# Group-norm statistics moved between slices, and the last image's loads regrouped, in a dilated attention and binary convolution kernel

## The chip, the cores and the metric

The kernel runs on one core of one Trainium2 chip. The metric is the device time of one execution in microseconds (us). A profiled execution has a span, from its first to its last instruction, and a time of its own that is a little longer. TensorE (PE in the profile) multiplies matrices, VectorE (DVE), ScalarE (ACT) and GpSimd (POOL) work elementwise, and SyncE (SP) issues most DMAs. PEld is TensorE's loading of weights.

## What is computed

Input and output are 16 images of 56 x 56 pixels with 384 channels in float32. Two layers follow each other, each with a group norm ahead of it and a residual around it:

```python
x = x + _L0_conv_ref(_gn(x), L0_conv_w_qkv, L0_conv_w_proj, L0_conv_b_proj)
x = x + _L1_conv_ref(_gn(x), L1_conv_w)
```

`_gn` takes mean and variance over all pixels of one image and the 12 channels of each of 32 groups. So no pixel of an image can be normalised before the whole image has been seen:

```python
g = v.reshape(B_, H_, W_, G, C_ // G)
m = jnp.mean(g, axis=(1, 2, 4), keepdims=True)
s = jnp.var(g, axis=(1, 2, 4), keepdims=True)
return ((g - m) / jnp.sqrt(s + eps)).reshape(v.shape)
```

Layer 0 projects to q, k and v (384 to 1152 channels), lets each pixel attend to 3 x 3 neighbours in 3 groups of 4 heads, with dilations 1, 2 and 3 in the groups, and projects back with a bias. Layer 1 is a depthwise 3 x 3 convolution whose weights are clipped and turned to their signs.

## The kernel before

The work is cut into 112 chunks of 8 image rows (448 pixels), 7 per image. Channels lie on the partitions, in three groups of 128. Each chunk passes three plans. `plan_a` loads the input, transposes it, takes its statistics and writes it channel by channel to the scratch tensor `xd`. `plan_b` is layer 0: it normalises, projects q, k and v, forms nine products t with the keys on VectorE (`score`, L516), sums them on TensorE, takes the softmax, spreads the weights with TensorE, multiplies with v on VectorE and adds on GpSimd (`weigh`, L586 and L594), projects, adds the residual, takes layer 1's statistics and stores to `x1d`. `plan_c` is layer 1: it loads `x1d`, normalises, convolves and transposes to the output.

The order is written out by hand. Each piece of work is entered with a slice and an order in it (`at`, L382), the pieces are emitted sorted by both (L836), and a chunk starts every 9 slices (`STEP`, L820). The orders are listed at L819; SOFTMAX, SCORE, CONVOLVE, WEIGH and QUERY stand ahead of STATISTICS, then come QKV, PROJECT, the transposes, NORM and LOADS. This is the order in which pieces are written; VectorE and GpSimd are seen to depart from it in the trace, where an instruction whose input comes late is passed by later ones. [...]

**Statistics.** `group_norm` (L295) returns six steps that lie in different slices: `channels` (VectorE combines the chunks' statistics, L305), `mean` (a matmul and a scaling, L311 and L314), `deviation` (matmuls, VectorE L323, GpSimd L324 and L325), `variance` (a matmul and three VectorE operations, L331 to L338), `invert` (thirteen small GpSimd operations that find the inverse square root, L345 to L349, and leave `pair`), and `spread_out` (matmuls `pp`, L354, bring mean and scale back to the channels; for layer 1 more matmuls `pz`, L367, bring them to the layout of the convolution; VectorE copies both to `mr`, L358, and `mrz`, L372). Only `channels` and `invert` have no matmul. For layer 1 the steps lie in slices 0, 1, 2, 4, 5 and 7 after slice 27 of the image's last chunk (L822, L649), for layer 0 at the same offsets from another start (L821, L443).

**Layer 1 in an image.** The first 256 channels are convolved on TensorE: z holds a set of 32 channels three times on 96 partitions, once for each of three image rows shifted (`load`, L669), there are 4 sets for each j of 2, ScalarE normalises z with `mrz` (L701), and twelve taps per j accumulate (`convolve`, L709). The last 128 channels, g, are multiplied by their taps on ScalarE (`taps_g`, L762) and added on GpSimd (L768), after ScalarE has normalised `xg` to `zg` with `mr` (L740). `turn` (L778) transposes to the output; ScalarE copies it to `osb`, and a DMA stores that.

**The last image.** It has no later image to share the engines with, so `plan_c` treats it apart (L675 to L680 and L790 to L804). z lies in halves of two sets, in tiles that layer 0 has no use for any more: `t` tiles for even chunks, three `w` tiles and one `xn` tile for odd ones. VectorE normalises the fourth set (L697) and does the taps of g alone (`taps_last`, L753). Loads of z are by image row and half, six for each j (L688). Loads of xg (L729), from a pool of two `xg` tiles, and of x1 (L707), from a pool of two `x1` tiles, are entered six slices ahead of the chunk; the loads of z follow five and four slices ahead. SP issues all of these in one queue. An xg or x1 tile is free again when the chunk two back has been transposed to the output.

## Time and profile before

The median of three runs is 5430.9 us (5424.45 to 5435.38).

| | us |
|---|---|
| Profiled execution, its own time | 5427.23 |
| its span | 5425.5 |
| mean granted TensorE clock | 0.976 |
| `invert`, GpSimd L345 / L346 / L347, mean of one (96 of each in all) | 0.195 / 0.211 / 0.188 |
| `channels`, VectorE L305, mean of one (96 in all) | 0.337 |
| L594, GpSimd add of w, mean of one | 3.05 |
| L768, GpSimd add of taps, mean of one | 3.05 |
| L586, VectorE product w, mean of one | 1.55 |
| z load for one image row (L688), issue to landing, median | 4.0 |
| z_last load (last image), issue to landing, median | 3.5 |
| x1 load (L707), issue to landing, median | 7.9 |

The profile's page gives the busy time of each engine, the span in 40 slices of 135.6 us, the DMA queues, the chain that ended last, and the costliest groups. Its busy time of TensorE includes matmuls that run slower because the granted clock is lower. A timeline lists instructions in order: start, duration, engine, line, operation, tiles, and in brackets how long the engine had been idle and what ended that. In a table of stretches each row has a stretch's bounds and length, the busy time of PE, PEld, DVE, ACT and POOL with their instructions, the granted clock, the busy share of the DMA engines and the GB/s they moved. A line of waits names who waited, for whom, and then the sum in us, how often, and the longest.

### The profile page before, as it was taken

Reading aid. Unit: us, or ns where it says so; the run is one execution under the profiler, and the core shown is the slowest. Engines: PE = TensorE matmul, PEld = TensorE weight load, DVE = VectorE, ACT = ScalarE, POOL = GpSimd, SP = SyncE. Lnnn points to the kernel's source line nnn. Section 1 sums busy time; section 2 is a strip of 40 time slices with the busy share of each in tenths; the row PEclk is TensorE's granted clock in tenths of the full one; section 3 lists DMA queues with packets and bytes.
Section 4 is the critical chain, followed back from the end, with each engine's and each line's share of the span. In section 5 each row is a group of like instructions: output and inputs, shape, how many; then the busy total and the mean of one; then the engine's idle time right before and its main releaser. Section 6 shows DMA issues by size and latency. Waiting matters only on the chain. (4 is left out here: it accounts for less than half of the span.)

```text
span 5425.5 us, 77496 instructions
## 1 busy us (share of the span) xinstructions
PE 5215.6 (96%) x27669; PEld 2430.9 (45%) x27669; DVE 4143.1 (76%) x4209; ACT 2400.9 (44%) x4189; POOL 4216.7 (78%) x3049
## 2 busy tenths in 40 slices
PE   8999999999999999999999999999999999999965
PEld 4444444444444444444444444444444444444422
DVE  4887777878777787778877777787778878777753
ACT  3224444444444444444444444444444444444433
POOL 2677888888787887888888888887888888888870
PEclk9999999999999999999999999999999999999976
DMA  5444555655556555555655555555555555545444
GB/s 167 126 119 124 160 158 152 164 153 161 154 158 162 164 156 161 159 158 152 163 153 160 155 160 161 162 156 161 159 158 153 164 152 160 155 134 134 128 120 129
DMA packets 811640, 825.75 MB, mean 152 GB/s; under 512 B 360307, under 2 KB 801014, under 8 KB 811254
## 3 DMA queue, kind: packets, MB, share of 16 engines
q1 hardware_dynamic: 803270, 808.79, 54.2%
q10 hardware_dynamic: 7984, 12.00, 0.7%
q8 instruction: 219, 3.59, 0.3%
q14 instruction: 167, 1.37, 0.1%
HBM read 466.41 MB, written 231.21 MB: 129 GB/s over the span
## 5 line engine op out<-in xcount | busy, mean ns | idle before, releaser
L594 POOL TENSOR_TENSOR w<-w 128x1344 f32<-128x1344 f32 x672 | 2049.9, 3050 | 461.3 <-DVE w L586 359.3
L586 DVE TENSOR_TENSOR w<-pb_a,v 128x1344 f32<-128x1344 f32 x1008 | 1560.3, 1548 | 246.4 <-PE pb_a L579 164.6
L516 DVE TENSOR_TENSOR t<-pq,k 128x1344 f32<-128x1344 f32 x1008 | 1535.1, 1550 | 247.0 <-PE pq L463 247.0
L463 PE MATMUL pkv<-xn,wqkvT 128*128 128x448 f32 x3924 | 1565.6, 548 | 0.0
L463 PEld LDWEIGHTS pkv<-xn,wqkvT 128*128 128x128 f32 x3924 | 717.8, 190 | 659.4 <-issue 631.1
L612 PE MATMUL po<-y,wprojT 128*128 128x448 f32 x2016 | 833.3, 550 | 19.6 <-POOL y L598 15.7
L768 POOL TENSOR_TENSOR m<-m 128x1344 f32<-128x1344 f32 x210 | 640.0, 3048 | 272.2 <-ACT m L762 272.2
L463 PE MATMUL pq<-xn,wqkvT 128*128 128x448 f32 x1962 | 826.7, 557 | 0.0
L701 ACT ACTIVATE z<-z,mrz 96x448 f32<-96x448 f32 x840 | 578.4, 751 | 435.8 <-DMA z<-x1d 407.2
L501 PE MATMUL ps<-t,sel 128*32 128x448 f32 x6048 | 678.3, 559 | 35.4 <-DVE t L516 34.8
L762 ACT ACTIVATE m<-zg,ktap 128x448 f32<-128x448 f32 x945 | 554.0, 658 | 285.0 <-POOL m L768 278.0
L612 PEld LDWEIGHTS po<-y,wprojT 128*128 128x128 f32 x2016 | 376.3, 191 | 373.8 <-issue 343.5
L715 PE MATMUL pc<-z,kdiag 96*32 96x440 f32 (+1 forms) x5040 | 528.9, 554 | 6.1 <-POOL z L703 4.4
L722 DVE TENSOR_TENSOR x<-pc,x 128x448 f32<-128x448 f32 x224 | 139.8, 624 | 461.4 <-PE pc L715 461.3
L463 PEld LDWEIGHTS pq<-xn,wqkvT 128*128 128x128 f32 x1962 | 345.4, 189 | 311.3 <-issue 311.3
L579 PE MATMUL pb_a<-aT,spread 24*128 24x448 bf16 x3024 | 369.3, 360 | 41.0 <-DVE w L586 35.7
L598 POOL TENSOR_TENSOR y<-y,w 128x448 f32<-128x448 f32 x336 | 381.4, 1135 | 22.6
L597 POOL TENSOR_TENSOR y<-w 128x448 f32<-128x448 f32 x336 | 381.9, 1137 | 14.7
L473 ACT COPY v<-pkv 128x448 f32<-128x448 f32 x336 | 178.6, 531 | 474.5 <-PE pkv L463 466.2
L615 DVE SCALAR_TENSOR_TENSOR xr<-po,bias,xr 128x448 f32<-128x448 f32 x336 | 227.7, 678 | 187.3 <-PE po L612 183.4
L473 ACT COPY k<-pkv 128x448 f32<-128x448 f32 x336 | 178.2, 530 | 371.0 <-PE pkv L463 371.0
L501 PEld LDWEIGHTS ps<-t,sel 128*32 128x32 f32 x6048 | 172.4, 111 | 378.9 <-issue 250.4
(128 smaller groups left out, 4406.2 us busy)
## 6 DMA issues: line engine op xcount, KB each, us to landing
z<-x1d SPq DMA_DIRECT2D x570, 224.0 KB, 4.0
xr<-xd SPq DMA_DIRECT2D x112, 672.0 KB, 4.3
x1d<-xr SPq DMA_DIRECT2D x112, 672.0 KB, 3.2
xn<-xd SPq DMA_DIRECT2D x109, 672.0 KB, 4.6
xin<-in_x_dram SPq DMA_DIRECT2D x108, 672.0 KB, 7.1
xd<-xa SPq DMA_DIRECT2D x315, 224.0 KB, 3.5
out_dram<-osb SPq DMA_DIRECT2D x420, 168.0 KB, 3.4
x<-x1d SPq DMA_DIRECT2D x112, 448.0 KB, 7.9
```

What stands on the lines that cost most here:

```text
L463: nc.tensor.matmul(dst[:, :PX], wqkvT[:, cc, o0 : o0 + P], had["xn"][:, cc, :], start=(cc == 0), stop=(cc == NG - 1))
L501: return nc.tensor.matmul(had["ps"][32 * j : 32 * j + 32, :PX], sel[:, s0 : s0 + 32], tk, start=(issued[j] == 1), stop=(issued[j] == len(r ...
L516: nc.vector.tensor_tensor(t.rearrange("p k (r w) -> p k r w", w=W), q3, k3, ALU.mult)
L586: nc.vector.tensor_tensor(w.rearrange("p k (r w) -> p k r w", w=W), pb[:, :, :PX].rearrange("p k (r w) -> p k r w", w=W), three(kv[1][g][m ...
L594: nc.gpsimd.tensor_tensor(w0, w0, w, ALU.add)
L597: nc.gpsimd.tensor_tensor(y, w0[:, 0], w0[:, 1], ALU.add)
L598: nc.gpsimd.tensor_tensor(y, y, w0[:, 2], ALU.add)
L612: nc.tensor.matmul(po[:, :PX], wprojT[:, g, j * P : (j + 1) * P], had[f"y{g}"], start=(g == 0), stop=(g == NG - 1))
L701: nc.scalar.activation(z, z, AF.Identity, bias=mrz[:, j, q, 0:1], scale=mrz[:, j, q, 1:2])
L715: return nc.tensor.matmul(pcr[q * HD : (q + 1) * HD, :, lo:hi], kdiag[:, kx, j * NQ + q, :], rows(set_of(j, q))[:, :, lo + kx - 1 : hi + k ...
L762: nc.scalar.activation(rows(t[:, kx]), zp[:, ky : ky + ROWS, kx : kx + W], AF.Copy, scale=ktap[:, o : o + 1])
L768: nc.gpsimd.tensor_tensor(had["m"], had["m"], t, ALU.add)
```

## The change

Four things are changed. The orders gain one: STATISTICS now stands ahead of CONVOLVE, and a new order SPREAD stands where it was. `channels` and `invert` get STATISTICS, the four steps with matmuls get SPREAD, for both layers. The last step for layer 1, `spread_out`, lies one slice sooner. In the last image the load of x1 is entered three slices later, xg lies in an `xn` tile (of which there are three), and the half of odd chunks that lay in an `xn` tile lies in the `xr` tile. And in the last image's chunks 1 to 5 z is loaded by sets: one DMA brings all three image rows of a set, so there are four DMAs for each j where there were six. Its first and last chunk are loaded as before.

```diff
@@ plan_a
             for k in range(6):
-                at(t0 + 5 + STAT0_SLICE[k], STATISTICS, lambda k=k: norm(k))
+                at(t0 + 5 + STAT0_SLICE[k], STAT_ORDER[k], lambda k=k: norm(k))
@@ plan_b
             for k in range(6):
-                at(t0 + 27 + STAT1_SLICE[k], STATISTICS, lambda k=k: norm(k))
+                at(t0 + 27 + STAT1_SLICE[k], STAT_ORDER[k], lambda k=k: norm(k))
@@ plan_c, load
                 for q0 in range(0, NQ, 2):
-                    pool, tag = (t_p, "t") if c % 2 == 0 else (w_p, "w") if (j, q0) != (1, 2) else (xn_p, "xn")
+                    pool, tag = (t_p, "t") if c % 2 == 0 else (w_p, "w") if (j, q0) != (1, 2) else (xr_p, "xr")
...
                 for z, q0, q1 in had[f"z{j}"]:
+                    if b == B - 1 and 0 < c < NCH - 1:
+                        continue
                     nc.sync.dma_start(
                         z[ky * HD : (ky + 1) * HD, :, lo:hi], by_set[:, q0:q1, n0 + lo : n0 + hi]
                     )
+            if b == B - 1 and 0 < c < NCH - 1:
+
+                for q in range(NQ):
+                    one = by_set[:, q, p0 - W : p0 - W + PX]
+                    three_rows = bass.AP(one.tensor, one.offset, [(W, 3), *one.ap])
+                    nc.sync.dma_start(set_of(j, q), three_rows)
@@ plan_c, load_g
-            had["xg"] = xg = xg_p.tile([P, ROWS + 2, W], F32, tag="xg", name="xg")
+            if b < B - 1:
+                had["xg"] = xg = xg_p.tile([P, ROWS + 2, W], F32, tag="xg", name="xg")
+            else:
+                xg = xn_p.tile([P, NG, PX], F32, tag="xn", name="xg_last").rearrange("p j n -> p (j n)")
+                had["xg"] = xg = rows(xg[:, : (ROWS + 2) * W])
@@ plan_c, last image
             at(t0 - 6, LOADS, load_g)
-            at(t0 - 6, LOADS, load_x)
+            at(t0 - 3, LOADS, load_x)
@@ orders
-    SOFTMAX, SCORE, CONVOLVE, WEIGH, QUERY, STATISTICS, QKV, PROJECT, STAGE_A, STAGE_C, NORM, LOADS = range(12)
+    SOFTMAX, SCORE, STATISTICS, CONVOLVE, WEIGH, QUERY, SPREAD, QKV, PROJECT, STAGE_A, STAGE_C, NORM, LOADS = range(13)
+
+    STAT_ORDER = (STATISTICS, SPREAD, SPREAD, SPREAD, STATISTICS, SPREAD)
     STEP = 9
     STAT0_SLICE = (0, 1, 2, 4, 5, 7)
-    STAT1_SLICE = (0, 1, 2, 4, 5, 7)
+    STAT1_SLICE = (0, 1, 2, 4, 5, 6)
```

## The prediction

> **What bounds the kernel now.** I read the page first (busy shares, 40 slices), then the stretches by engine, then TensorE's waits in the middle, then the timeline around one of them, and last the DMA queue's waits in the end.

> ```profile
> span 5425.5 us, 77496 instructions
> ...
> PE 5215.6 (96%) x27669; PEld 2430.9 (45%) x27669; DVE 4143.1 (76%) x4209; ACT 2400.9 (44%) x4189; POOL 4216.7 (78%) x3049
> ...
> PE   8999999999999999999999999999999999999965
> ...
> PEclk9999999999999999999999999999999999999976
> ...
> 2848.00:3179.00 331.00, 326.08 (x1754) 153.01 (x1753) 259.54 (x263) 153.96 (x270) 271.95 (x192) 0.99 0.57 157
> ...
> 5320.00:5340.00 20.00, 11.96 (x60) 5.98 (x60) 8.24 (x13) 6.88 (x12) 0.00 (x0) 0.58 0.49 141
> ```

> In the middle TensorE (the first engine column of a stretch) is busy 98.5%; there, only less TensorE idling or a better granted clock (third column from the end) is time. In the last two slices every engine idles and the clock is near half. So there are two purses: the idling once per image, and the end.

> ```profile
> PE ps L501 <- DVE t L516: 29.4, 22, 2.0
> PE pb_a L579 <- DVE w L586: 24.3, 14, 7.1
> PE pv L331 <- POOL dev L325: 10.9, 14, 0.9
> ```
> ```profile
> 1131.91 0.37 PE L579 MATMUL pb_a<-aT,spread 24*128 24x448 bf16 x3 [1.34 <-DVE w L586]
> ...
> 1134.84 3.21 PE L501 MATMUL ps<-t,sel 128*32 128x448 f32 x16 [2.02 <-DVE t L516]
> ```
> ```profile
> 1134.86:1138.27 3.41, 3.41 (x20) 0.97 (x24) 1.93 (x2) 2.19 (x4) 2.70 (x2) 0.50 0.98 285
> ```

> From 100 to 5000 us TensorE waits some 75 us, 54 of them in the first two lines, at one place per image. The pair of 1.34 and 2.02 us, 3.36 us in sum, comes once in each of 13 images (the first has one wait of 7.1 us), always followed by a stretch at half clock: 3.41 us in nine images, 6.83 in four. At half rate half of it is lost: (9 x 3.41 + 4 x 6.83) / 2 / 13 = 2.2 us. One such place costs 5.6 us, and 13 cost 73.

> Its cause lies 30 us before. The timeline has ScalarE idle 4.50 us at 1101.66 for `mr` (the copy at L358 behind the spreading's matmuls), so the new image's `zg`, the taps L762 and GpSimd's L768 start late (GpSimd idle 2.32 us at 1109.19). GpSimd then runs behind; VectorE waits 3.16 us at 1130.30 for its w tile, and TensorE for VectorE.

> ```profile
> 1091.52 0.36 PE L579 MATMUL pb_a<-aT,spread 24*128 24x448 bf16 x3
> ...
> 1098.98 0.72 PE L354 MATMUL pp<-pair,gselT 32*128 32x2 f32 x6
> ```
> ```profile
> 1094.23 0.18 POOL L349 TENSOR_TENSOR pair<-pair 32x1 f32<-32x1 f32 x1
> ```
> ```profile
> SPq L729 <- PE pt_o L783: 49.5, 6, 11.4
> ```
> ```profile
> 5345.09 4.88 PE L715 MATMUL pc<-z_last,kdiag 96*32 96x448 f32 x24 [7.72 <-DVE z_last L697]
> ```

> The first three of these lines (timeline of TensorE and of GpSimd) give the slack of the spreading: `pair` is complete at 1094.41, the spreading runs at 1098.98, and the slice before begins on TensorE at 1091.52. The last two show the end (5296 to 5400): SP waits 49.5 us in six pieces, with the load of xg at its head, for the output transposes of the chunk two back, whose xg and x1 buffers it wants. The z loads stand behind it in the same queue, and TensorE waits for them, about 7 us a chunk.

> [...]here z_last takes 3.5 us at the median and 5 to 6 us in the end, so latency counts there and issuing early hides it.

> **The change part by part.** Sums are against the profiled execution, 5427.2 us (span 5425.5); the runs' median, 5430.9, is 3.7 above.

> *Channels and invert first in their slices.* The first is 3 aggregates of 0.34 us on VectorE; at worst they delay one w product by 1.0 us, and TensorE has other work queued. The second is 13 small GpSimd operations, 3.5 us. In the trace the chain already runs ahead of its slice's w add (layer 0: 888.78 to 892.45, the add at 893.53), and for layer 1 nothing but two edge memsets competes in slice 5. So 0; bounds +1 and -1 us per image.

> *Layer 1's spreading one slice sooner.* It moves 54 tiny matmuls (0.72 + 0.68 us) and two VectorE copies ahead of twelve k and v matmuls (4.8 us) and one output projection (2.4 us); no DMA is moved by it. TensorE keeps the written slice order everywhere I looked, so `pp` would stand directly after the pb_a of 1091.52, thus at 1091.9, and `pair` comes at 1094.4: a new wait of 2.6 us. Behind it stand those k and v matmuls, for which ScalarE's copies wait, and nothing else is short. If instead the instruction order that the compiler settles on puts the matmuls of k and v first, the wait is 0. No row shows this wait, so these are its two bounds. I take 2.6, since `pv` waits 0.87 us for GpSimd in just that manner instead of letting k and v pass.

> What it buys: `mr` some 4 us sooner by the clock (1097.6 at the latest, when VectorE has finished its two products, against 1101.5). GpSimd's first L768 can start when it is free of the sums of y, at 1106.9 for 1109.2: 2.3 us. With the wait at `pp`, TensorE itself comes 2.6 us later too, so GpSimd's lag of 3.16 us at 1130 is gone but for some 0.3 us of idling. Clock: [...] about 6 times in 10: 0.6 x 1.7 = 1.1 us.
> Per image: before 5.6; after 2.65 + 0.3 + 1.1 = 4.05; gain 1.5 us, 13 times = 20 us. In the first image `pair` is done 2.2 us before `pp`, and `mr` gains about 2.5 us of the 7.1: 2.5. Without the new wait: 2.3 idling and 2.2 clock = 4.5 per image, 58 us, and 5 in the first.

> *Last image.* xg in xn tiles (three, idle by then), x1's load three slices later and so behind the z loads: SP no longer stops z. Six loads per j become four in chunks 1 to 5 (12 to 8 per chunk, at 0.45 us: 1.8 us of issue, off the path once loads run ahead). The xr tile for one w-parity half is free after the store that lands at 5266.9, 40 us before use. What is late next? Per chunk: TensorE at half clock 4.88 + 4.88 + 2.2 (transposes) = 12.0 us; ScalarE 6 x 0.75 + 0.85 + 4 x 0.48 + 4 DMA issues of 0.35 = 8.7 plus waits for the two osb buffers, 2 to 3 us (1.75 and 0.54 in one chunk); VectorE 9 x 0.69 + 2 x 0.62 + 2 x 0.5 = 8.5. x1, now later, lands 5 to 6 us after its issue, while the first convolution lasts 4.9: covered but for 1 us. I take 12 us per chunk, bounds 10.5 (full clock, ScalarE) and 15 (osb waits in full).
> Now: the second chunk's convolution starts at 5308.8, 8.5 us after TensorE was free; the starts from there to the last chunk's, at 5396.7, are 87.9 us apart. After: 8.5 saved and 5 x 12 = 60: 36.4 us saved. The last chunk's own 28.8 us stay. Bounds: 44 and 21.

> Sum: 5427.2 - 20 - 2.5 - 36.4 = 5368.3; on the runs' median 5372.

> **Rivals.**
> *No new wait* (TensorE fills the gap with k and v): 58 + 5 + 36.4 = 99 off, 5332 by the median. For: VectorE and GpSimd are seen out of written order, so order bends to readiness. Against: TensorE never is outside the end.
> *The spreading gains nothing, the end does*: its wait takes the old one's place with the same clock loss: 5431 - 36 = 5395. For: 2.6 of 3.4 us is taken at once. Against: TensorE's lateness is itself GpSimd's relief.
> *Slower*: the wait at `pp` starts a half-clock stretch in every image, and the old pair of waits stays, since the taps' L768 still alternates with ScalarE for two m buffers: 14 x (2.65 + 1.7) = 61 lost, less 36 in the end = 25 over, 5456. It decides once an image loses over 36 / 14 = 2.6 us net, which is the wait at `pp` in full with nothing bought. For: the alternation (1.75 us) is in every chunk. Against: ScalarE's 4.5 us wait for `mr` is what differs in these chunks.
> *The end stays*: the SP order keeps x1 ahead of z, or ScalarE's output waits replace it: about 20 of the 36 us are gone. It is in the range.

> **How the numbers follow.** The forecast 0.40; no new wait 0.30; end only 0.17; slower 0.09; neither end nor middle moves, within 0.2% (11 us, what a measurement of this kernel can tell), 0.04. Faster 0.87, same 0.04, slower 0.09. From the forecast with its bounds (+13 and -40) and the rivals to either side: 5322 to 5412.

> **What would show it.** Spreading: a wait of `pp` for `pair`, some 2.6 us in some 14 images, ScalarE's wait for `mr` under 1.5 us, and the waits of pb_a for w and ps for t down from 54 us to under 20; if pp never waits, the first rival. Clock: half-rate stretches in the middle from 13 to about 8. End: SP's wait at the xg load nearly gone, z landed before its convolution, chunk starts 12 us apart, last chunk's start near 5340. Wrong: the old pair of waits unchanged, or chunk starts still 19 us apart.

## The result, and the profile after

The changed kernel takes 5445.7 us, the median of four runs, against 5432.5 us for the kernel before on the same chip: a ratio of 1.0026 with a 95% interval of 1.0009 to 1.0044. It is slower by 13 us where 59 us less were forecast. All medians here leave out executions in the chip's slower state, of which there was one, 5550.7 us in e1_rows. The changed kernel's profiled execution took 5440.49 us, against 5427.23. Lines of the changed kernel are numbered higher: z_last is loaded at L690 (rows) and L698 (sets), x1 at L715, xg at L741; VectorE's part of z_last is L705, ScalarE's L709, the convolution L723.

The page of the changed kernel: span, busy time, TensorE in 40 slices, the clock, and the chain that ended last by line.

```profile
span 5438.4 us, 77423 instructions
...
PE 5233.3 (96%) x27669; PEld 2427.7 (45%) x27669; DVE 4141.7 (76%) x4209; ACT 2407.6 (44%) x4189; POOL 4213.1 (77%) x3049
...
PE   8999999999999999999999999999999999999965
...
PEclk8999999999999999999999999999999999999966
...
DMA z_last<-x1d 2%; PE pc L723 0%; SPq L698 0%; DMA out_dram<-osb 0%; ACT osb L797 0%; ACT z_last L709 0%; PE pt_o L795 0%; DVE m L765 0%; SPq L715 0%; SPq L800 0%; DVE z_last L705 0%; ACT zg L752 0%; DVE x L730 0%; ACTq L800 0%; POOL z_last L711 0%
```

The slices look nearly as before, so they don't tell where 13 us went. The chain points to the end: DMAs of `z_last` lead it with 2% of the span, about 100 us, and only the last image has such tiles. To split the difference by place I took the same VectorE instruction in both traces. The output projection's L615 near 404 us is 0.5 us later in the changed kernel; the add behind the convolution (L722, now L730), at 763.54 us before, is 11.8 us later; and the last L615 ahead of the last image's convolution is 2.3 us earlier, first in the kernel before and then in the changed one:

```profile
5262.22 0.69 DVE L615 SCALAR_TENSOR_TENSOR xr<-po,bias,xr 128x448 f32<-128x448 f32 x1 [0.33 <-PE po L612]
```
```profile
5259.95 0.68 DVE L615 SCALAR_TENSOR_TENSOR xr<-po,bias,xr 128x448 f32<-128x448 f32 x1 [0.56 <-PE po L612]
```

So the stretch with the first image's statistics loses 11.8 us (0.5 of it ahead of 404 us), the next thirteen images and the rest before the end win 14.1, and from -2.3 the end brings the shift to +13.3 (5440.49 - 5427.23): it loses 15.5 us.

**The middle.** TensorE's waits from 100 to 5000 us in the changed kernel (sum in us, times, longest). Here `pv` is the matmul of the variance, `ps` sums the products t, `pb_a` spreads the attention weights and `po` is the output projection:

```profile
PE pp L354 <- POOL pair L349: 42.6, 15, 5.2
PE pv L331 <- POOL dev L325: 11.3, 14, 0.9
PE ps L501 <- DVE t L516: 5.9, 9, 2.9
PE pb_a L579 <- DVE w L586: 5.0, 2, 4.9
```

The old pair, ps for t and pb_a for w, is down from 53.7 to 10.9 us. In its place TensorE waits at `pp`, once per image, right behind the pb_a that the forecast named (the changed kernel's timeline, then the half-clock stretch that follows, as a row of stretches with the clock third from the end):

```profile
1103.72 0.36 PE L579 MATMUL pb_a<-aT,spread 24*128 24x448 bf16 x3
1106.69 0.82 PE L354 MATMUL pp<-pair,gselT 32*128 32x2 f32 x6 [2.60 <-POOL pair L349]
```
```profile
1108.93:1112.34 3.41, 3.41 (x8) 1.06 (x6) 0.88 (x1) 0.24 (x1) 1.03 (x1) 0.50 0.00 0
```

Such a stretch follows in every image, 3.41 us in nearly all. GpSimd's timeline shows what `pair` waits for: two sums of y stand inside `invert`, which begins at 1101.20 and leaves `pair` at 1106.63.

```profile
1101.34 1.13 POOL L597 TENSOR_TENSOR y<-w 128x448 f32<-128x448 f32 x1
...
1102.58 1.12 POOL L598 TENSOR_TENSOR y<-y,w 128x448 f32<-128x448 f32 x1
```

The chain takes 5.4 us here, as it does with the same two sums in the kernel before (1088.99 to 1094.41). Without them `pair` would come some 2.2 us sooner, an estimate from these durations, and most of the 2.6 us would go; no run tried it.

In the first image there are three waits where there was one of 7.1 us, and 23.9 us at half clock for 10.2:

```profile
443.19 1.44 PE L354 MATMUL pp<-pair,gselT 32*128 32x2 f32 x6 [5.17 <-POOL pair L349]
...
474.42 3.19 PE L501 MATMUL ps<-t,sel 128*32 128x448 f32 x16 [2.88 <-DVE t L516]
...
493.10 0.56 PE L579 MATMUL pb_a<-aT,spread 24*128 24x448 bf16 x3 [4.87 <-DVE w L586]
```

**The end.** Waits from 5296 to 5420 us in the changed kernel, all for the loads of z:

```profile
DVE z_last L705 <- DMA z_last<-x1d: 62.0, 10, 9.2
ACT z_last L709 <- DMA z_last<-x1d: 47.7, 21, 5.8
PE pc L723 <- DVE z_last L705: 46.1, 9, 8.0
```

SP's wait at the xg load, 49.5 us before, is gone as forecast. But SP's timeline (SPq in the view) has the eight loads of one chunk in its queue for 17.84 us (changed kernel), where the twelve loads by rows of a chunk took 8.95 (kernel before):

```profile
5324.66 17.84 SPq L698 DMA_DIRECT2D z_last<-x1d  x8
```
```profile
5318.11 8.95 SPq L688 DMA_DIRECT2D z_last<-x1d  x12
```

From 5327.40 to 5330.00 us the changed kernel has nothing but loads by sets under way. There the 16 DMA engines are busy 0.20 of the time and move 74 GB/s; 0.20 x 16 = 3.2, so as an estimate from that share about three engines carry these loads. From 5320 to 5340 us the share is 0.41 at 138 GB/s, with loads by rows 0.75 at 213 GB/s (e1_rows, below).

The packets under 512 B set the loads apart too. In e1_rows, where no load is by sets, 1744 such packets stand against 108 DMAs from 5300 us on, which is 16 each with one DMA more that was under way. From 5286.4 us on, the changed kernel's DMA view has:

```profile
DMA packets 11111, 17.50 MB, mean 114 GB/s; under 512 B 969, under 2 KB 10720, under 8 KB 11104
...
z_last<-x1d SPq DMA_DIRECT2D x39, 168.0 KB
out_dram<-osb ACTq DMA_DIRECT2D x28, 168.0 KB
x<-x1d SPq DMA_DIRECT2D x6, 448.0 KB
z_last<-x1d SPq DMA_DIRECT2D x8, 112.0 KB
xg_last<-x1d SPq DMA_DIRECT2D x3, 280.0 KB
out_dram<-osb SPq DMA_DIRECT2D x3, 168.0 KB
z_last<-x1d SPq DMA_DIRECT2D x4, 98.0 KB
xg_last<-x1d SPq DMA_DIRECT2D x1, 252.0 KB
```

The 53 DMAs that aren't by sets account for 53 x 16 = 848 small packets; 121 are left for the 39 loads by sets and one issued just before. That is three each, and one over, the number of engines that the busy share gave. The source of a load by sets has three image rows, `(W, 3)`, as its outermost dimension; that its three engines come from there was my estimate, and e5_set_parts below changes that dimension. Eight loads of 168 KB (1.376 MB) in 17.84 us are 77 GB/s, against the 213 of all DMAs with loads by rows.

The first convolutions of chunks 1 and 4 in the changed kernel:

```profile
5301.27 4.66 PE L723 MATMUL pc<-z_last,kdiag 96*32 96x448 f32 x24 [3.78 <-DVE z_last L705]
...
5366.97 4.66 PE L723 MATMUL pc<-z_last,kdiag 96*32 96x448 f32 x24 [5.42 <-DVE z_last L705]
```

From chunk to chunk that is (5366.97 - 5301.27) / 3 = 21.9 us; 12 were forecast.

### The profile page after: what moved, and what is told of

It is laid out like the page before. It is cut to its first block, busy times and chain, and to the rows that moved or that the text cites. A ratio compares the mean times of both kernels' runs of the same rounds, so it can differ in the third digit from the quotient of the medians.

```text
span 5438.4 us, 77423 instructions
## 1 busy us (share of the span) xinstructions
PE 5233.3 (96%) x27669; PEld 2427.7 (45%) x27669; DVE 4141.7 (76%) x4209; ACT 2407.6 (44%) x4189; POOL 4213.1 (77%) x3049
## 2 busy tenths in 40 slices
PE   8999999999999999999999999999999999999965
## 5 line engine op out<-in xcount | busy, mean ns | idle before, releaser
L586 DVE TENSOR_TENSOR w<-pb_a,v 128x1344 f32<-128x1344 f32 x1008 | 1559.8, 1547 | 249.1 <-PE pb_a L579 175.4
L516 DVE TENSOR_TENSOR t<-pq,k 128x1344 f32<-128x1344 f32 x1008 | 1536.5, 1550 | 245.6 <-PE pq L463 245.6
L463 PE MATMUL pkv<-xn,wqkvT 128*128 128x448 f32 x3924 | 1594.7, 555 | 0.0
L709 ACT ACTIVATE z<-z,mrz 96x448 f32<-96x448 f32 x840 | 580.1, 752 | 418.1 <-DMA z<-x1d 391.5
L501 PE MATMUL ps<-t,sel 128*32 128x448 f32 x6048 | 663.2, 548 | 10.6 <-DVE t L516 9.8
L723 PE MATMUL pc<-z,kdiag 96*32 96x440 f32 (+1 forms) x5040 | 517.4, 544 | 5.0 <-POOL z L711 4.4
L730 DVE TENSOR_TENSOR x<-pc,x 128x448 f32<-128x448 f32 x224 | 139.8, 624 | 427.3 <-PE pc L723 420.5
L579 PE MATMUL pb_a<-aT,spread 24*128 24x448 bf16 x3024 | 369.9, 360 | 21.9 <-DVE w L586 17.2
L615 DVE SCALAR_TENSOR_TENSOR xr<-po,bias,xr 128x448 f32<-128x448 f32 x336 | 227.8, 678 | 188.1 <-PE po L612 184.1
L424 ACT COPY xa<-pt_x 128x448 f32<-128x448 f32 x315 | 168.2, 534 | 384.1 <-PE pt_x L412 381.0
```

Of the source, the lines that this page charges most:

```text
L463: nc.tensor.matmul(dst[:, :PX], wqkvT[:, cc, o0 : o0 + P], had["xn"][:, cc, :], start=(cc == 0), stop=(cc == NG - 1))
L501: return nc.tensor.matmul(had["ps"][32 * j : 32 * j + 32, :PX], sel[:, s0 : s0 + 32], tk, start=(issued[j] == 1), stop=(issued[j] == len(r ...
L516: nc.vector.tensor_tensor(t.rearrange("p k (r w) -> p k r w", w=W), q3, k3, ALU.mult)
L586: nc.vector.tensor_tensor(w.rearrange("p k (r w) -> p k r w", w=W), pb[:, :, :PX].rearrange("p k (r w) -> p k r w", w=W), three(kv[1][g][m ...
L709: nc.scalar.activation(z, z, AF.Identity, bias=mrz[:, j, q, 0:1], scale=mrz[:, j, q, 1:2])
L723: return nc.tensor.matmul(pcr[q * HD : (q + 1) * HD, :, lo:hi], kdiag[:, kx, j * NQ + q, :], rows(set_of(j, q))[:, :, lo + kx - 1 : hi + k ...
```

## The experiments

Each kernel was timed in turns with the kernel before, whose medians in the four rounds were 5432.5, 5428.8, 5426.2 and 5429.1 us (one round for the changed kernel, one for the e runs, one for v1 to v4, one for v7, x8 and x9). The last column is the difference of the two medians of a round.

| kernel | median us | ratio to before, 95% | us |
|---|---|---|---|
| changed kernel | 5445.7 | 1.0026 [1.0009, 1.0044] | +13.2 |
| e1_rows: changed, z by rows | 5397.2 | 0.9945 [0.9931, 0.9958] | -31.6 |
| e2_sets_only: before, z by sets | 5444.5 | 1.0033 [1.0020, 1.0045] | +15.8 |
| e3_stat_undone: changed, old statistics | 5442.4 | 1.0028 [1.0017, 1.0039] | +13.6 |
| e5_set_parts: changed, sets in three loads | 5406.4 | 0.9958 [0.9944, 0.9971] | -22.3 |
| v3_tail_only: e1, old statistics | 5396.8 | 0.9942 [0.9930, 0.9955] | -29.4 |
| v4_order_slice7: e1, spreading in slice 7 | 5396.7 | 0.9943 [0.9930, 0.9955] | -29.5 |
| v2_first7: e1, first image in slice 7 | 5385.0 | 0.9922 [0.9909, 0.9934] | -41.2 |
| v1_late: e1, spreading behind k and v | 5348.1 | 0.9857 [0.9841, 0.9873] | -78.1 |
| v7_late_pv: v1, layer 0's steps later | 5345.6 | 0.9848 [0.9835, 0.9862] | -83.6 |
| x8_xg_only: before, xg in xn tiles | 5412.5 | 0.9970 [0.9960, 0.9981] | -16.6 |
| x9_x1_only: before, x1 later | 5417.9 | 0.9981 [0.9975, 0.9988] | -11.3 |

### Is it the three engines?

My theory for the end was that the loads by sets are slow because of their three engines; the rival was that the new order of SP's queue is at fault.

**e1_rows** takes the loads by sets out of the changed kernel.

```diff
-                    if b == B - 1 and 0 < c < NCH - 1:
-                        continue
                     nc.sync.dma_start(
...
-                for q in range(NQ):
-                    one = by_set[:, q, p0 - W : p0 - W + PX]
-                    three_rows = bass.AP(one.tensor, one.offset, [(W, 3), *one.ap])
-                    nc.sync.dma_start(set_of(j, q), three_rows)
```

> The changed kernel with the last image's z loaded by image row again; everything else of the change stays. Theory 'three rings' (a load by sets is carried by only three of the sixteen DMA engines, so each chunk's eight loads need some 19 us): with the rows back the end gains what was forecast, about 50 us against the changed kernel, near 5395; DVE's and ACT's waits for z_last fall from 62 and 48 us to under 15, chunk starts come 12 to 13 us apart. Rival 'order of the queue' (the later x1 load or xg in other tiles is what holds up the end): no more than 5 us gained, near 5440, and the waits for z_last stay above 40 us.

Measured: 32 us faster than before and some 45 us faster than the changed kernel. From 5296 to 5420 us VectorE's and ScalarE's waits for loads of z are down from 62.0 and 47.7 us to 9.0 and 4.8. The convolutions of chunks 2 and 5 (e1_rows, timeline of TensorE):

```profile
5320.59 8.28 PE L714 MATMUL pc<-z_last,kdiag 96*32 96x448 f32 x46 [3.51 <-ACT z_last L700]
...
5362.21 7.76 PE L714 MATMUL pc<-z_last,kdiag 96*32 96x448 f32 x48 [3.80 <-ACT z_last L700]
```

The chunks are now 13.9 us apart, (5362.21 - 5320.59) / 3, somewhat over the 12 to 13 that were expected, and TensorE waits mainly for ScalarE's normalising instead of for loads. The rival falls: x1 and xg are loaded here as in the changed kernel.

**e2_sets_only** puts the same loads by sets into the kernel before, with nothing else.

> The kernel before with nothing but the loads by sets in the last image's chunks 1 to 5. Theory 'three rings': the loads take 13 us instead of 3.5 to 6, added to the queue's old waits for the output transposes: slower than before by 15 to 40 us (5447 to 5472). Rival 'order of the queue': within 5 us of before, 5427 to 5437.

16 us slower: clearly a loss, at the lower edge of what was expected. Part of the loads' length takes the place of SP's old waits: from 5296 to 5420 us SP waits 8.3 us for output transposes here, 49.5 in the kernel before.

**e5_set_parts** keeps the order by sets but gives each row its own load, so that the outermost dimension is 32 channels.

```diff
-                    one = by_set[:, q, p0 - W : p0 - W + PX]
-                    three_rows = bass.AP(one.tensor, one.offset, [(W, 3), *one.ap])
-                    nc.sync.dma_start(set_of(j, q), three_rows)
+                    for ky in range(3):
+                        n0 = p0 + (ky - 1) * W
+                        nc.sync.dma_start(set_of(j, q)[ky * HD : (ky + 1) * HD], by_set[:, q, n0 : n0 + PX])
```

> The changed kernel with each load by sets cut into three loads of 32 partitions, the same bytes in the same order of sets, 24 loads per chunk for 8. Theory 'three rings': 32 channels spread over all sixteen engines, each load lands in 3 to 6 us, and the end gains as with rows, 5395 to 5410 (24 issues of 0.45 us are 10.8 us per chunk, close under the 12 us of TensorE, so up to 15 us worse than with rows). Rival 'the bytes or the packets themselves are slow': no gain, near 5445. Rival 'SP is short of issue time': slower than the changed kernel.

36 us faster than the changed kernel, with three times as many DMAs for the same bytes. From 5300 us on 166 DMAs leave 2656 packets under 512 B, 16 each, these loads too, where a load by sets left three. One chunk's 24 loads in SP's queue, from e5_set_parts:

```profile
5327.11 14.16 SPq L698 DMA_DIRECT2D z_last<-x1d  x24
```

They take less time than the eight of the changed kernel, and a load lands in 2.1 us at the median. So neither the bytes nor the order by sets is slow, but the shape of the access pattern, with which a load's small packets go from three to 16. It is 9 us slower than loads by rows; the 24 issues may be why, which wasn't tried.

### What the statistics are worth

**e3_stat_undone** is the changed kernel with the old order and slice.

```diff
-    STAT_ORDER = (STATISTICS, SPREAD, SPREAD, SPREAD, STATISTICS, SPREAD)
+    STAT_ORDER = (SPREAD,) * 6
-    STAT1_SLICE = (0, 1, 2, 4, 5, 6)
+    STAT1_SLICE = (0, 1, 2, 4, 5, 7)
```

> The changed kernel with the order and slices of the statistics' steps as before; the last image as changed. If the statistics are worth what the shift between the two traces says (a loss of 11 us in the first image, a gain of 1.1 us in each of 13 more, so about 3 us in sum): 5448, 1 to 5 us over the changed kernel. If the traces mislead and the middle is what got slower: below 5440. The middle shows the old pair of waits (pb_a for w and ps for t, some 54 us) and no wait of pp.

13.6 us over before, as with the statistics changed (13.2): in sum they are worth nothing that can be told. **v3_tail_only** makes the same edit with loads by rows.

> The kernel before with only xg in xn tiles, x1's load three slices later and one half of z in the xr tile: loads by rows, statistics as before. If the end is worth what was forecast (36 us) and the statistics nothing in sum (-11 us in the first image, +14 after): 5431 - 33 = 5398, the same as with the statistics changed, 5394 to 5403. If the statistics' change is a net loss: below 5390.

29.4 us faster, e1_rows 31.6: again nothing in sum that can be told. The end by itself is worth 29 us, where 36 were forecast.

**v4_order_slice7** leaves the new order and takes only the second half of that edit, slice 7.

> The changed kernel with loads by rows and the spreading back in slice 7, so that of the statistics only the order within the slices (channels and invert first) is changed. Forecast for that part: nothing (within 1 us per image), so like the last image's change alone, 5395 to 5402. Rival 'the order costs or brings something by itself': outside 5385 to 5412; then some of the first image's 11 us or the later gain of 1.1 us per image belongs to the order and not to the slice.

It can't be told from v3_tail_only (29.5 and 29.4): putting `channels` and `invert` first in their slices costs and brings nothing. The two sums of y still stood inside layer 1's `invert` in the changed kernel, so that the chain itself hadn't become shorter.

**v2_first7** keeps slice 6 for all images but the first.

```diff
-                at(t0 + 27 + STAT1_SLICE[k], STAT_ORDER[k], lambda k=k: norm(k))
+                at(t0 + 27 + STAT1_SLICE[k] + (b == 0 and k == 5), STAT_ORDER[k], lambda k=k: norm(k))
```

> The changed kernel with loads by rows, and the spreading left in slice 7 for the first image only. The traces say that the first image loses 11 us by the move (pp waits 5.2 us there, and some 24 us run at half clock for 10): 5398 - 11 = 5387. If the first image's loss has another cause (STATISTICS ahead of the convolutions, say): 5398.

10 us less than e1_rows, where 11 were expected: the first image's loss is the spreading's new place there, and the other images gain the 12 us that v2_first7 has over v3_tail_only.

**v1_late** keeps slice 6 and writes the spreading behind that slice's k and v matmuls, by an order LATE between QKV and PROJECT.

```diff
-                at(t0 + 27 + STAT1_SLICE[k], STAT_ORDER[k], lambda k=k: norm(k))
+                at(t0 + 27 + STAT1_SLICE[k], STAT_ORDER[k] if k < 5 else LATE, lambda k=k: norm(k))
```

> The changed kernel with loads by rows, and layer 1's spreading kept in slice 6 but written behind the k and v matmuls of that slice instead of ahead of them. Theory 'the wait at pp eats the gain': TensorE has 4.8 us of matmuls before pp, pair is ready (2.6 us short before), so the wait of pp and the half-clock stretch behind it go, while mr still comes 2 us sooner than in the kernel before: about 2.6 + 1.7 us per image off 14 images against loads by rows alone (5398), 60 us, near 5340; at least 30 us. Rival 'the place of pp is indifferent, the taps' buffers set GpSimd's lag': the old pair of waits (pb_a for w, ps for t) comes back, 54 us, and the time stays within 10 us of 5398.

5348.1 us: 47 less than e1_rows against the kernel before of its round, 78 less than the kernel before, so this version beats both kernels. Its waits of TensorE from 100 to 5000 us, and `pp` in one image:

```profile
PE pb_a L579 <- DVE w L586: 11.5, 14, 0.9
PE pv L331 <- POOL dev L325: 11.5, 13, 0.9
PE po L612 <- ACT k L473: 9.8, 11, 1.7
PE ps L501 <- DVE t L516: 8.2, 10, 4.2
...
PE pp L354 <- POOL pair L349: 0.5, 1, 0.5
```
```profile
1086.78 4.78 PE L463 MATMUL pkv<-xn,wqkvT 128*128 128x448 f32 x12
1091.49 0.82 PE L354 MATMUL pp<-pair,gselT 32*128 32x2 f32 x6
```

The k and v matmuls, 4.78 us, now stand where TensorE waited 2.6. Between 100 and 5000 us two half-clock stretches are left, of 6.8 and 3.4 us, where the changed kernel had 17. They come to 10.2 us, the half-clock stretches of v3_tail_only to 68.2; half of the difference, 29 us, is the clock's share of the gain, as an estimate from these sums. ScalarE's wait for `mr` at zg, in the changed kernel and in v1_late:

```profile
1107.75 0.81 ACT L752 ACTIVATE zg<-xg,mr 128x504 f32<-128x504 f32 x1 [10.01 <-DVE mr L358]
```
```profile
1092.64 0.81 ACT L743 ACTIVATE zg<-xg,mr 128x504 f32<-128x504 f32 x1 [0.52 <-DVE mr L358]
```

**v7_late_pv** moves layer 0's last three steps one slice later as well, against the wait of pv for dev.

```diff
-                at(t0 + 5 + STAT0_SLICE[k], STAT_ORDER[k], lambda k=k: norm(k))
+                at(t0 + 5 + (STAT0_SLICE[k] + (b > 0 and k >= 3)), STAT_ORDER[k], lambda k=k: norm(k))
```

> Loads by rows and the spreading behind k and v, and in addition layer 0's variance, invert and spreading one slice later in all images but the first. It takes away the one wait of TensorE that is left in every image in the middle, pv for dev, 0.88 us in 14 images: 12 us off 5348, so 5336. Nothing is late next, since xn is normalised with that mr0 more than 60 slices later. If TensorE's saved wait is taken up by another engine's (VectorE and GpSimd are at 78%): 5343 to 5350.

The wait of pv went, and the time hardly moved: 5345.6, a miss by 10 us; against the kernel before of each round it is 5 us better than v1_late. TensorE's wait of po for ScalarE's k went from 9.8 to 16.0 us, pp waited 3.0 for 0.5, and the half-clock stretches between 100 and 5000 us grew from 10.2 to 20.5 us, half of which is lost. These three give 14 us back, more than the 11.5 us that pv had waited.

### Which edit of SP's queue gains

x8_xg_only is v3_tail_only with x1's load back in its old place, and x9_x1_only is the kernel before with only this load moved.

```diff
 x8_xg_only, against v3_tail_only
-            at(t0 - 3, LOADS, load_x)
+            at(t0 - 6, LOADS, load_x)
 x9_x1_only, against the kernel before
-            at(t0 - 6, LOADS, load_x)
+            at(t0 - 3, LOADS, load_x)
```

> The kernel before with xg in xn tiles (and one half of z in the xr tile), but x1's load still six slices ahead, in front of the z loads. Theory: an x1 and an xg tile become free by the same output transposes, two chunks back, so either of the two at the head of the queue stops the z loads just as long, and one edit alone gains under 8 us (5420 to 5431). Rival: the two edits add, about half of the 30 us each, 5410 to 5416.

> The kernel before with only x1's load three slices later; xg from its pool of two as before, at the head of the queue. Theory: xg alone stops the z loads as long as both did, gain under 8 us (5420 to 5431). Rival: the two edits add, 5410 to 5416.

Here my theory fell: 16.6 and 11.3 us, 28 together, against 29.4 for both. The parts add, though x9_x1_only, at 5417.9, lies a little over what the rival had for it. SP's waits for output transposes from 5296 to 5420 us show them, 49.5 us before; x8_xg_only, then x9_x1_only:

```profile
SPq L706 <- PE pt_o L786: 28.4, 5, 8.3
```
```profile
SPq L729 <- PE pt_o L783: 38.1, 5, 11.4
```

With one of the two loads out of the way the wait is shorter, though the other still stands ahead of z. Why it shortens so evenly wasn't tried.

## Why the prediction was wrong

Against its sum for the profiled execution, 5368.3, the changed kernel took 5440.49. The 72 us divide into three terms.

*Last image: 52 of the 72 us, and the step that failed.* The text has "Six loads per j become four in chunks 1 to 5 (12 to 8 per chunk, at 0.45 us: 1.8 us of issue, off the path once loads run ahead)". It counted DMAs and their issue, and took the landing time of the loads by rows for loads of another shape. Eight loads occupied SP for 17.84 us instead of 3.6, with some three of the DMA engines busy where such loads were alone (0.20 of 16), and the end lost 15.5 us where it should have saved 36.4. The two other edits of the end were forecast well: with loads by rows they save 29 us, chunks 13.9 us apart for 12, inside the bounds of 10.5 and 15. The rival "the end stays" named other causes, SP's order and ScalarE's output waits; neither applied.

*First image: 14 us.* The text said "In the first image `pair` is done 2.2 us before `pp`, and `mr` gains about 2.5 us of the 7.1". That 2.2 us was the slack at the old place. The move brings `pp` forward by 4.8 + 2.4 = 7.2 us, so the same subtraction as for the other images would have given a wait of 5.0 us; 5.17 was measured. With the clock lost behind it, 11.8 us of loss stood in place of a gain of 2.5, and v2_first7 gives 10 of it back.

*The other images: 6 us.* The mechanism was right in its place, its 2.6 us, and in the vanishing of the old pair. The mis-sized term is the clock, "6 times in 10: 0.6 x 1.7 = 1.1 us", where the 6 in 10 was my estimate and no trace had shown it. The half-clock stretch came in every image, 1.7 us (17 stretches in the middle where about 8 were forecast), and the gain was about 1.1 us per image instead of 1.5.

*Channels and invert first:* nothing, as forecast (v4_order_slice7). But "nothing but two edge memsets competes in slice 5" was misread: two sums of y, 2.25 us, lay inside layer 1's `invert` in the kernel before too, so that it took 5.4 us and not 3.5. The sum didn't suffer, since it took the time of `pair` from the trace.

*The rivals by their sums.* "The spreading gains nothing, the end does" comes within 3 us of e1_rows, the change without its loads by sets (5395 for 5397.2), but by luck: its wait didn't take the old one's place at the same cost; a gain of 14.1 us and a loss of 11.8 cancelled. "Slower" came true for the changed kernel by another cause than its own: the half clock came in every image as it said, but the old pair of waits went, and the end, which it counted as a gain of 36, lost 15.5.

*"No new wait"* didn't happen in the changed kernel, but v1_late makes it happen: 49 us below v3_tail_only, where the rival had 63. Its mechanism holds, and it was the better part of what the spreading had to give. *The sign of ScalarE's wait for `mr`* was forecast wrongly too: it was to fall under 1.5 us and rose to 10 in the changed kernel, from 61.0 to 153.5 us in sum. It costs little by itself, as far as the trace tells: ScalarE's next work there, the v copy at 1112.10, waits 3.54 us more for matmuls that stand behind `pp`.

## What to carry to other kernels

Before merging loads into fewer, look at the shape of the access pattern and not only at the number of DMAs: here three by 32 by 448 ran at 77 GB/s, and 32 by 448 three times over was faster with three times the issues. When a step on TensorE moves ahead to serve others, take its wait out of every case separately, the first iteration too, and put work that is ready ahead of it: here the same slice with 4.8 us of k and v matmuls in front gained 49 us where the plain move gained nothing. An edit that loses can hide one that gains; time the parts alone.

## What the runs showed of the hardware

**Half clock after less than 2 us of idling.** At 440 and again at 4993 us in the changed kernel half clock began when TensorE had idled for 1.9 us. In v1_late one gap of 1.74 us, at 4082, was followed by half clock; one of 1.60 us at 4826 wasn't, nor was any of its 27 waits of up to 0.9 us at `pb_a` and `pv`. No limit can be read from this. Where the 2.6 us at `pp` were split by a step of the grid, 1.66 and 0.94 us near 3051 us, the granted clock was 1.00 behind that step, until 3054.53, and 0.50 only behind the next. The idle times are those of TensorE and its weight loads with modelled ends.

**SP spent longer on the issue of a load by sets.** The issue of one load by sets took SP 1.2 us at the median and up to 4.0 (changed kernel, L698), that of one by rows 0.38 and at most 0.54 (kernel before, L688, in the end). What stood behind in the queue was slow as well: the issue of x1, which isn't by sets, took 2.61 us at 5320.59 in the changed kernel, and 0.40 at 5317.66 in the kernel before.
